# Four graph-attention layers in float32: the token transposes of layers 1 and 3 taken from TensorE and done as 32x32 block transposes plus block moves

## The chip, the core and the metric

The kernel runs on one core of a Trainium2 chip. The metric is device time in microseconds (us). A core has a matrix engine (TensorE, PE in the profile), a vector engine (VectorE, DVE), a scalar engine (ScalarE, ACT), a general engine (GpSimd, POOL) and a queue engine (SyncE, SP) that here only issues transfers. [...]

## The reference, cut to what matters

128 graphs of 64 nodes, 512 features each, so 8192 rows of 512 floats. Four layers, each of the form `x = x + layer(relu(layernorm(x)))`:

```python
# layers 0, 2: 4 heads of 64, one adjacency mask per graph
out = softmax(where(adj, (h@Wq)(h@Wk)^T / 8, -max)) @ (h@Wv);   x += out @ Wo + bo
# layer 1: a second layernorm with gamma and beta, 8 heads of 64
h2 = layernorm(h) * gamma + beta;   the same attention with w_qkv;   x += out @ w_out.T + b_out
# layer 3: m = h @ map_w.T + map_b; q, k from m; 8 heads
adj3 = (cosine(m, m) * keep > 0.1) * softmax(q k^T / 8, masked)
x += relu(((adj3 @ (h @ gcn_map_w.T + gcn_map_b)) @ gcn_W.T) / (adj3.sum(-1) + 1))
```

A projection contracts over features, so TensorE needs the normalised tokens with features on the partitions. The transposes of this study turn `h` from tokens-on-partitions into features-on-partitions.

## The kernel before, in words

**Tiling.** P is 128, D 512, TB 4, NC 4. The rows are cut into 16 groups of 512 rows (four blocks of 128 tokens). A *step* `(l, s)` is layer `l` on group `s`, and the steps run in the order of `[(l, s) for l in range(4) for s in range(16)]`. All data is float32.

**A step.** `loads` brings a group in as two halves of 256 rows, each into a tile `xin` of 128x2x512 out of a ring of four. `layernorms` normalises each half in place: `scales` computes mean and variance on DVE (lines 443, 445, 448, 452) and the power on POOL (450), and `normalize` applies them with one ACT instruction per 128 tokens (459); layer 1 does both twice. `transposes` then makes `hT`, 128x4x512, out of a ring of two (`r_h`). After it, `sums_of_b` (line 366 on POOL, four instructions) forms the four sums `T` of quarters of `hT`, in one of three tiles of the bank `t` (`r_t`); the same bank holds the sums `oT_T` of the attention output and `mT_T` of layer 3's map output.

**Projections.** Each is a Winograd-Strassen product of seven partial products, in `winograd`, with line 585 as its only matmul. The order of the seven is p, q, p, r, p, r, p: the PSUM bank `mA` (p) is used four times, and each use needs the evacuation of the one before by ACT (lines 602, 606, 622, 1012) to have ended. Between two uses of p lies one product in another bank (`mB` or `mC`). The first two products read `hT` itself, the third needs `T`. Layer 1 has four such units a step (q, k, v, and the output projection o), layer 3 has map, sem, q and k.

**Transposes before.** Line 539 (layers 0, 2, 3) and line 516 (layer 1, in `scaled_chunks`) transpose one 128x128 block each on TensorE into the PSUM tile `ptr`, sixteen a step. Four fill one tile. ACT copies it to `hT`: at line 544 as it is, at line 521 with layer 1's gamma and beta as scale and bias. That makes four ACT instructions a step.

**The attention** already holds a transposition without TensorE, in `transposed`: eight ACT copies (line 946) move 32-partition blocks of the weights `E` to the place that they have in the transposed matrix, and one DVE instruction (line 951) transposes every 32x32 block where it stands.

**Order.** Nothing is scheduled by hand. The kernel's generators say before each instruction which engine it takes and for how long by an assumed cost (`yield act(0.6)`), `Order.run` walks through them as an event simulation with priorities, and the instructions are written in the order in which that simulation starts them. `Order.urgent` lets an evacuation (priority 0 or less) go ahead of lower work on ACT and DVE that would still be running when it becomes ready. So an edit to one helper can move every instruction around it.

Of the kernel before, what the change touches and what calls it, by code (L numbers as in the profile page):

```python
# [10 lines left out]
AF = mybir.ActivationFunctionType  # L11
# [3 lines left out]
P = 128  # L15
D = 512
N = 64
TB = 4
NC = D // P
# [184 lines left out]
def pe(us):  # L204
    return ("pe", us, 0.25)
# [18 lines left out]
def load(us=2.2):  # L224
    return ("sp", 0.6, us)
# [3 lines left out]
def gnn_stack(ctx: ExitStack, tc: tile.TileContext, a: dict, out: bass.AP):  # L229
    nc = tc.nc  # L230
    x_d = a["x"]
    NG = x_d.shape[0] // (P * TB)
    od = Order()

    def ring(tag, n, shape, dtype=F32, space=None):
        kw = {} if space is None else {"space": space}
        p = ctx.enter_context(tc.tile_pool(name=tag, bufs=n, **kw))
        return Ring(od, p, n, shape, dtype, tag)

    def bank(tag, n, shape, dtype=F32):  # L240
        return Bank(od, ctx.enter_context(tc.tile_pool(name=tag, bufs=1)), n, shape, dtype, tag)
# [3 lines left out]
    soft = ctx.enter_context(tc.tile_pool(name="soft", bufs=3))  # L245
    dram = ctx.enter_context(tc.tile_pool(name="dram", bufs=1, space=bass.MemoryType.DRAM))
    r_w = ring("w", 4, [P, 7, 2, H])
    r_xin = ring("xin", 4, [P, 2, D])
    r_xres = ring("xres", 2, [P, 2, D])
    r_u = bank("u", 4, [P, D])  # L250
    r_h = ring("h", 2, [P, NC, TB * P])
    r_t = bank("t", 3, [P, NC, 2, H])
# [13 lines left out]
    r_tr = ring("tr", 2, [P, NC, P], space=ps)  # L266
# [4 lines left out]
    def x_of(layer, s):  # L271

        return x_d[s * TB * P:(s + 1) * TB * P, :] if layer == 0 else xs[layer - 1][s]


    ident = const.tile([P, P], F32, name="ident")
# [21 lines left out]
    gamma, beta, map_b, q_b, k_b, gcn_b = (vecs[:, i, :] for i in range(6))  # L298
# [40 lines left out]
    o_taken, o_done = od.event(), od.event()  # L339
# [97 lines left out]
    def scales(v):  # L437

        mv = small.tile([P, 2, 2], F32, tag="mv", name="mv")
        for t in range(2):  # L440
            st = small.tile([P, 6], F32, tag="st", name="st")
            yield dve(0.68)
            nc.vector.bn_stats(st, v[:, t, :])  # L443
            yield dve(0.17)
            nc.vector.bn_aggr(mv[:, t, :], st)
        rs = small.tile([P, 3, 2], F32, tag="rs", name="rs")
        yield dve(0.25)
        nc.vector.tensor_scalar_add(rs[:, 1, :], mv[:, :, 1], LN_EPS)  # L448
        yield pool(0.75)
        nc.gpsimd.tensor_tensor(rs[:, 0, :], rs[:, 1, :], mhalf[:, :2], ALU.pow)  # L450
        yield dve(0.45)
        nc.vector.scalar_tensor_tensor(rs[:, 2, :], mv[:, :, 0], -1.0, rs[:, 0, :],  # L452
                                       ALU.mult, ALU.mult)
        return rs

    def normalize(v, rs, func):
        for t in range(2):
            yield act(0.81)
            nc.scalar.activation(v[:, t, :], v[:, t, :], func, bias=rs[:, 2, t:t + 1],  # L459
                                 scale=rs[:, 0, t:t + 1])  # L460

    hT, hB, h_ready, h_done, t_done = {}, {}, {}, {}, {}

    def quarters(v):

        return lambda j, k: v[:, 2 * j:2 * j + 2, k * H:(k + 1) * H]

    loaded, l_ready = {}, {}

    def loads(steps):  # L470
        for l, s in steps:
            if l > 0:
                yield x_done[l - 1, s]
            for half in range(2):
                v, e = yield from r_xin.new()
                loaded[l, s, half] = v, e

                if (l, s) == (0, 1):
                    if half == 0:
                        yield begun_w  # L480
                    yield ("actq", 0.5, 0.0)
                else:
                    yield load(3.9)
                (nc.scalar if (l, s) == (0, 1) else nc.sync).dma_start(
                    v, x_of(l, s)[half * H:(half + 1) * H, :].rearrange("(t p) d -> p t d", p=P))
                if (l, s) == (0, 1):
                    if half == 1:
                        loads_begun.set()
                    yield ("actq", 0.0, 8.0)
                l_ready[l, s, half].set()  # L490

    normed, n_ready = {}, {}

    def layernorms(steps, half):

        for l, s in steps:
            yield l_ready[l, s, half]
            x, xe = loaded.pop((l, s, half))
            rs = yield from scales(x)
            yield from normalize(x, rs, AF.Relu)  # L500
            if l == 1:
                rs = yield from scales(x)
                yield from normalize(x, rs, AF.Identity)
            normed[l, s, half] = x, xe
            n_ready[l, s, half].set()

    def scaled_chunks(s, h):

        for half in range(2):
            yield n_ready[1, s, half]  # L510
        x = [normed.pop((1, s, half)) for half in range(2)]
        for c in range(NC):
            pt, pe_ = yield from r_tr.new("ptr")
            for b in range(TB):
                yield pe(0.115)
                nc.tensor.transpose(pt[:, b, :], x[b // 2][0][:, b % 2, c * P:(c + 1) * P], ident)  # L516
            if c == NC - 1:
                for _, xe in x:
                    xe.set()
            yield act(0.6)  # L520
            nc.scalar.activation(h[:, c, :], pt.rearrange("p b k -> p (b k)"), AF.Identity,  # L521
                                 bias=beta[:, c:c + 1], scale=gamma[:, c:c + 1])
            pe_.set()

    def transposes(steps):

        for l, s in steps:
            h, h_done[l, s] = yield from r_h.new("hT")
            hT[l, s] = h
            if l == 1:  # L530
                yield from scaled_chunks(s, h)
            for half in range(2 if l != 1 else 0):
                yield n_ready[l, s, half]
                x, xe = normed.pop((l, s, half))
                for t in range(2):
                    pt, pe_ = yield from r_tr.new("ptr")
                    for c in range(NC):
                        yield pe(0.115)
                        nc.tensor.transpose(pt[:, c, :], x[:, t, c * P:(c + 1) * P], ident)  # L539
                    if t == 1:  # L540
                        xe.set()
                    yield act(0.6)
                    b = 2 * half + t
                    nc.scalar.copy(h[:, :, b * P:(b + 1) * P], pt)  # L544
                    pe_.set()
                if (l, s, half) == (0, 0, 0):
                    yield from has_h(l, s, h)
            if (l, s) == (3, 1):
                yield o_taken
            if (l, s) != (0, 0):  # L550
                yield from has_h(l, s, h)
            yield from sums_of_b(quarters(h), hB[l, s][1], (l, s) == (0, 0))
            hB[l, s][2].set()
            if (l, s) == (0, 0):
                first_t.set()

    def has_h(l, s, h):
        T, t_done[l, s] = yield from r_t.new("T")
        hB[l, s] = (quarters(h), T, od.event())
        h_ready[l, s].set()  # L560
# [746 lines left out]
```

## Time and profile before

| | before |
|---|---|
| time, median of 3 runs | 2819.91 us (2817.82 to 2821.30) |
| the profiled execution: time / its span | 2823.6 us / 2821.8 us |
| PE busy | 2766.3 us, 98% |
| PE weight loads busy | 2398.8 us, 85% |
| DVE busy | 1822.2 us, 65% |
| ACT busy | 1679.4 us, 60% |
| POOL busy | 1539.3 us, 55% |
| mean granted TensorE clock | 0.995 |
| moved by DMA | 238.56 MB, mean 85 GB/s |

The span is the time from the first to the last recorded instruction; the profiled execution took 1.8 us more than its span, and 3.7 us more than the median of the runs. Busy times of different engines overlap. TensorE's matmuls are pipelined, so the recorded durations of two neighbours overlap too, and what one matmul takes from TensorE is better read as the distance between starts.

### The profile page before, as it was taken

What the parts mean: (1) busy time and instruction counts of PE and PEld (TensorE: products, weight loads), DVE (VectorE), ACT (ScalarE), POOL (GpSimd) and SP (SyncE); (2) the same over time, 40 slices, a digit from 0 to 9 for tenths busy, and PEclk for the clock granted to TensorE, in tenths of its full rate; (3) what the DMA queues carried; (4) which work ended last, traced back from release to release, by engine and by line L of the source; (5) the groups of instructions that cost most, each with busy time, mean ns of one, the idle gap of its engine ahead of it and who ended that gap; (6) DMA issues with size and microseconds to landing.
All of it is one profiled execution on the core that took longest, in us unless ns stands there. A gap on an engine that the chain in (4) does not pass through costs nothing.

```text
span 2821.8 us, 64271 instructions
## 1 busy us (share of the span) xinstructions
PE 2766.3 (98%) x27176; PEld 2398.8 (85%) x27176; DVE 1822.2 (65%) x2724; ACT 1679.4 (60%) x2841; POOL 1539.3 (55%) x1158
## 2 busy tenths in 40 slices
PE   8999999999999999999999999999999999999997
PEld 7888888888888888888889888888888888888876
DVE  6776676776665666655756667646666666665557
ACT  5666666667555755755656657655555555555444
POOL 5676667553444443335565576686545545455443
PEclk9999999999999999999999999999999999999998
DMA  4243233220211111212242233333222322222221
GB/s 156 92 136 100 98 114 129 80 91 29 80 46 69 54 61 47 76 61 77 79 136 99 99 122 107 107 121 85 70 63 82 88 77 62 63 78 75 65 63 46
DMA packets 160433, 238.56 MB, mean 85 GB/s; under 512 B 23953, under 2 KB 69009, under 8 KB 160145
## 3 DMA queue, kind: packets, MB, share of 16 engines
q1 hardware_dynamic: 145632, 219.98, 24.5%
q10 hardware_dynamic: 14512, 14.47, 1.6%
q8 instruction: 214, 3.51, 0.5%
q14 instruction: 75, 0.61, 0.1%
HBM read 166.77 MB, written 67.63 MB: 83 GB/s over the span
## 4 chain that ended last, share of the span: by engine, by line
PE 90%; DVE 4%; POOL 3%; ACT 1%; issue 1%; DMA 1%; POOLq 0%; ACTq 0%; SPq 0%; DVEq 0%
PE mA L585 44%; PE mC L585 22%; PE mB L585 11%; PE sc L902 5%; PE ptr L539 3%; PE po L1069 2%; PE po L1214 1%; PE ptr L516 1%; ACT F L946 1%; POOL t L366 1%; POOL xres L996 1%; PE mmn L844 1%; DVE t L363 1%; POOL E L937 1%; POOL xres L1017 1%
## 5 line engine op out<-in xcount | busy, mean ns | idle before, releaser
L946 ACT COPY F<-E 32x512 f32<-32x512 f32 x768 | 472.5, 615 | 53.7 <-POOL E L937 43.0
L1017 POOL TENSOR_TENSOR xres<-xres,u 128x512 f32<-128x512 f32 x192 | 249.3, 1305 | 207.1 <-ACT u L1012 162.5
L996 POOL TENSOR_TENSOR xres<-xres,u 128x512 f32<-128x512 f32 x192 | 257.0, 1360 | 88.3 <-DMA xres<-x 41.1
L459 ACT ACTIVATE xin<-xin,rs 128x512 f32<-128x512 f32 x320 | 248.6, 811 | 16.7 <-DVE rs L452 15.0
L366 POOL TENSOR_TENSOR t<-hT 128x512 f32<-128x512 f32 x126 | 170.6, 1354 | 144.0 <-ACT hT L544 82.8
L937 POOL TENSOR_TENSOR E<-E,sm 128x1024 f32<-128x1024 f32 x64 | 128.4, 2006 | 201.3 <-DVE sm L935 156.2
L443 DVE BATCH_NORM_STATS2 st<-xin 128x6 f32<-128x512 f32 x320 | 215.2, 672 | 30.1 <-DMA xin<-x 14.3
L602 ACT COPY v<-mA 128x256 f32<-128x256 f32 (+1 forms) x192 | 92.1, 480 | 215.6 <-PE mA L585 201.5
L450 POOL TENSOR_TENSOR rs<-rs,mhalf 128x2 f32<-128x2 f32 x160 | 122.9, 770 | 170.4 <-DVE rs L448 128.8
L585 PE MATMUL mA<-w_vo,t 128*128 128x128 f32 (+1 forms) x1152 | 204.6, 311 | 0.8 <-ACT v L602 0.6
L366 POOL TENSOR_TENSOR t<-hT,t 128x512 f32<-128x512 f32 x126 | 169.7, 1347 | 35.4 <-ACT hT L521 32.2
L585 PE MATMUL mA<-t,w_qk 128*128 128x256 f32 x768 | 185.2, 380 | 2.4 <-DVE t L363 1.4
L931 DVE TENSOR_REDUCE sm<-E 128x16 f32<-128x1024 f32 x128 | 155.2, 1212 | 42.3 <-ACT E L924 41.7
L585 PE MATMUL mA<-t,w_q 128*128 128x256 f32 x744 | 181.2, 380 | 0.9 <-ACT qT L602 0.9
L585 PEld LDWEIGHTS mA<-w_vo,t 128*128 128x128 f32 x1152 | 166.5, 191 | 13.0 <-ACT u L1012 1.8
L585 PE MATMUL mA<-t,w_k 128*128 128x256 f32 x744 | 177.4, 381 | 0.0
L585 PEld LDWEIGHTS mA<-t,w_qk 128*128 128x128 f32 x768 | 142.9, 190 | 21.2 <-issue 1.7
L585 PEld LDWEIGHTS mA<-t,w_k 128*128 128x128 f32 x744 | 140.3, 190 | 19.3
L585 PEld LDWEIGHTS mA<-t,w_q 128*128 128x128 f32 x744 | 137.7, 190 | 20.2 <-issue 2.5
L951 DVE STREAM_TRANSPOSE pt<-F 128x1024 f32<-128x1024 f32 x96 | 118.6, 1235 | 50.5 <-ACT F L946 50.4
L1012 ACT COPY u<-mA 128x512 f32<-128x512 f32 x144 | 84.4, 586 | 107.9 <-PE mA L585 102.2
L937 POOL TENSOR_TENSOR E<-E,f 128x1024 f32<-128x1024 f32 x32 | 63.8, 1994 | 129.9 <-DVE nz L965 65.0
(216 smaller groups left out, 6863.7 us busy)
## 6 DMA issues: line engine op xcount, KB each, us to landing
x<-xres SPq DMA_DIRECT2D x96, 512.0 KB
xin<-x SPq DMA_DIRECT2D x96, 512.0 KB
xres<-x SPq DMA_DIRECT2D x64, 512.0 KB
xres<-in_x SPq DMA_DIRECT2D x32, 512.0 KB
u<-rs SPq DMA_DIRECT2D x128, 128.0 KB
xres<-x SPq DMA_DIRECT2D x64, 256.0 KB
out<-xres SPq DMA_DIRECT2D x64, 256.0 KB
xin<-in_x SPq DMA_DIRECT2D x30, 512.0 KB
```

The lines of the kernel that those rows point to most:

```text
L366: nc.gpsimd.tensor_tensor(o, i0, i1, ALU.subtract)
L443: nc.vector.bn_stats(st, v[:, t, :])
L450: nc.gpsimd.tensor_tensor(rs[:, 0, :], rs[:, 1, :], mhalf[:, :2], ALU.pow)
L459: nc.scalar.activation(v[:, t, :], v[:, t, :], func, bias=rs[:, 2, t:t + 1], scale=rs[:, 0, t:t + 1])
L585: nc.tensor.matmul(o, l, r, start=(first and m == 0 and k == 0), stop=(k == KC - 1), skip_group_check=True)
L902: nc.tensor.matmul(S[g * N:(g + 1) * N, par, col], lT[r, c, k], rT[r, c, k], start=True, stop=True)
L931: nc.vector.tensor_reduce(o, E, AX.X, ALU.add)
L937: nc.gpsimd.tensor_mul(E, E, sm[:, :, None].to_broadcast([P, 16, N]))
L946: nc.scalar.copy(F[g * N + 32 * k:g * N + 32 * (k + 1), :, 32 * i:32 * (i + 1)], E[g * N + 32 * i:g * N + 32 * (i + 1), :, 32 * k:32 * (k ...
L951: nc.vector.transpose(o, F)
L996: nc.gpsimd.tensor_add(xr[:, t, :], xr[:, t, :], bo[l])
L1017: nc.gpsimd.tensor_add(v, v, both(u))
```

## The change

For steps 2 to 15 of layers 1 and 3 (28 of the 64 steps) the new generator `turned_tokens` takes the place of the TensorE transposes:

- It takes a tile of the bank `t` as soon as `hT` is allocated, and uses it first as a staging tile `F` and afterwards as the tile `T` of the sums.
- Sixteen copies of 32 partitions x 512 elements move each block row and block column of the 512x512 group to its transposed place in `F`: three of them on GpSimd, thirteen on ScalarE.
- Two VectorE instructions of 128x1024 transpose all 32x32 blocks from `F` into `hT`.
- In layer 1 four ScalarE instructions of 128x512 then apply gamma and beta to `hT` in place.

`scaled_chunks` is gone. Steps 0 and 1 of layer 1 now go through the general loop with line 544's plain copy, which applies no gamma and beta (these inputs are ones and zeros). The input ring becomes two tiles of 128x4x512 for a whole group, with one release for both halves, in place of four half tiles. The wait of step (3, 1) on `o_taken` in `transposes` moves into `turned_tokens`, which that step doesn't enter; `map_part` keeps its own.

```diff
-    r_xin = ring("xin", 4, [P, 2, D])
+    r_xin = ring("xin", 2, [P, TB, D])
...
-                v, e = yield from r_xin.new()
-                loaded[l, s, half] = v, e
+                if half == 0:
+                    x, e = yield from r_xin.new()
+                v = x[:, 2 * half:2 * half + 2, :]
+                loaded[l, s, half] = x, e
...
-    def scaled_chunks(s, h):
+    def turned_tokens(l, s):
         for half in range(2):
-            yield n_ready[1, s, half]
...
+            yield n_ready[l, s, half]
+        if (l, s) == (3, 1):
+            yield o_taken
+        h, h_done[l, s] = yield from r_h.new("hT")
+        hT[l, s] = h
+        x, xe = normed.pop((l, s))
+        T, t_done[l, s] = yield from r_t.new("T")
+        F = T.rearrange("p c a n -> p c (a n)")
+        xv = x.rearrange("p b (c k f) -> p k c b f", c=NC, k=4)
+        Fv = F.rearrange("p c (b i f) -> p i c b f", b=TB, i=4)
+        blocks = [(i, k) for k in range(4) for i in range(4)]
+
+        def part(pairs, done):
+            for i, k in pairs:
+                o, v = Fv[32 * k:32 * (k + 1), i], xv[32 * i:32 * (i + 1), k]
+                if done:
+                    yield pool(0.9)
+                    nc.gpsimd.tensor_copy(o, v)
+                else:
+                    yield act(0.615)
+                    nc.scalar.copy(o, v)
+            if done:
+                done.set()
+        moved = od.event()
+        od.spawn(part(blocks[:3], moved), 3)
+        yield from part(blocks[3:], None)
+        yield moved
+        xe.set()
+        for c in range(0, NC, 2):
+            yield dve(1.25)
+            nc.vector.transpose(h[:, c:c + 2, :], F[:, c:c + 2, :])
+        if l == 1:
+            for c in range(NC):
+                yield act(0.787)
+                nc.scalar.activation(h[:, c, :], h[:, c, :], AF.Identity,
+                                     bias=beta[:, c:c + 1], scale=gamma[:, c:c + 1])
+        hB[l, s] = (quarters(h), T, od.event())
+        h_ready[l, s].set()
+        return h
...
         for l, s in steps:
-            h, h_done[l, s] = yield from r_h.new("hT")
-            hT[l, s] = h
-            if l == 1:
-                yield from scaled_chunks(s, h)
-            for half in range(2 if l != 1 else 0):
+            if (l, s) in [(1, 2), (1, 3), (1, 4), (1, 5), (1, 6), (1, 7), (1, 8), (1, 9), (1, 10), (1, 11), (1, 12), (1, 13), (1, 14), (1, 15), (3, 2), (3, 3), (3, 4), (3, 5), (3, 6), (3, 7), (3, 8), (3, 9), (3, 10), (3, 11), (3, 12), (3, 13), (3, 14), (3, 15)]:
+                h = yield from turned_tokens(l, s)
+            else:
+                h, h_done[l, s] = yield from r_h.new("hT")
+                hT[l, s] = h
...
-            if (l, s) == (3, 1):
-                yield o_taken
```

More of the change, by code (lines that the diff above doesn't have):

```diff
@@ L497, in layernorms @@
             yield l_ready[l, s, half]
-            x, xe = loaded.pop((l, s, half))
+            whole, xe = loaded.pop((l, s, half))
+            x = whole[:, 2 * half:2 * half + 2, :]
             rs = yield from scales(x)
@@ L503, in layernorms @@
                 yield from normalize(x, rs, AF.Identity)
-            normed[l, s, half] = x, xe
+            normed[l, s] = whole, xe
             n_ready[l, s, half].set()
-    def scaled_chunks(s, h):
+    def turned_tokens(l, s):
         for half in range(2):
-            yield n_ready[1, s, half]
[L511 to L523, printed above, removed]
+            yield n_ready[l, s, half]
[36 more added lines that the diff above has]
+        return h
@@ L533, in transposes @@
+            for half in range(0 if (l, s) in [(1, 2), (1, 3), (1, 4), (1, 5), (1, 6), (1, 7), (1, 8), (1, 9), (1, 10), (1, 11), (1, 12), (1, 13), (1, 14), (1, 15), (3, 2), (3, 3), (3, 4), (3, 5), (3, 6), (3, 7), (3, 8), (3, 9), (3, 10), (3, 11), (3, 12), (3, 13), (3, 14), (3, 15)] else 2):
                 yield n_ready[l, s, half]
-                x, xe = normed.pop((l, s, half))
+                x, xe = normed[l, s]
                 for t in range(2):
+                    b = 2 * half + t
                     pt, pe_ = yield from r_tr.new("ptr")
@@ L538, in transposes @@
                         yield pe(0.115)
-                        nc.tensor.transpose(pt[:, c, :], x[:, t, c * P:(c + 1) * P], ident)
-                    if t == 1:
+                        nc.tensor.transpose(pt[:, c, :], x[:, b, c * P:(c + 1) * P], ident)
+                    if b == TB - 1:
                         xe.set()
                     yield act(0.6)
-                    b = 2 * half + t
                     nc.scalar.copy(h[:, :, b * P:(b + 1) * P], pt)
@@ L547, in transposes @@
                     yield from has_h(l, s, h)
-            if (l, s) == (3, 1):
-                yield o_taken
-            if (l, s) != (0, 0):
+            if (l, s) != (0, 0) and (l, s) not in [(1, 2), (1, 3), (1, 4), (1, 5), (1, 6), (1, 7), (1, 8), (1, 9), (1, 10), (1, 11), (1, 12), (1, 13), (1, 14), (1, 15), (3, 2), (3, 3), (3, 4), (3, 5), (3, 6), (3, 7), (3, 8), (3, 9), (3, 10), (3, 11), (3, 12), (3, 13), (3, 14), (3, 15)]:
                 yield from has_h(l, s, h)
```

## The prediction

> **What bounds the kernel now.** I read the page's busy times first, then the stages, then the rows of the touched work, then TensorE's timeline.
>
> ```profile
> span 2821.8 us, 64271 instructions
> PE 2766.3 (98%) x27176; PEld 2398.8 (85%) x27176; DVE 1822.2 (65%) x2724; ACT 1679.4 (60%) x2841; POOL 1539.3 (55%) x1158
> ```
>
> TensorE is busy for all but 55.5 us. Recorded busy can hide stalls, so look at the two stages in which the change lies (stretch, its length, then busy us of PE, PE loads, DVE, ACT, POOL):
>
> ```profile
> 466.00:1262.00 796.00, 794.94 (x7145) 689.75 (x7144) 503.08 (x789) 489.82 (x749) 357.38 (x280) 1.00 0.19 65
> 2030.00:2780.00 750.00, 745.42 (x7975) 629.02 (x7974) 463.04 (x622) 415.58 (x775) 377.68 (x252) 1.00 0.24 67
> ```
>
> The first holds the transposes of layer 1's sixteen steps (49.75 us each), the second most of layer 3. In both no engine but TensorE is over 64% busy. TensorE's timeline in layer 1 (start, us, engine, line, tiles, count) then tells what a transpose takes from it:
>
> ```profile
> 466.42 0.60 PE L516 MATMUL ptr<-ident,xin 128*128 128x128 f32 x4
> 466.85 1.46 PE L585 MATMUL mA<-t,w_qk 128*128 128x256 f32 x6
> ...
> 473.42 0.60 PE L516 MATMUL ptr<-ident,xin 128*128 128x128 f32 x4
> 473.86 1.06 PE L585 MATMUL mC<-w_vo,t 128*128 128x128 f32 x8
> ...
> 708.21 1.89 PE L585 MATMUL mC<-t,w_q 128*128 128x256 f32 x8
> 709.94 1.89 PE L585 MATMUL mA<-t,w_q 128*128 128x256 f32 x8
> 711.67 1.89 PE L585 MATMUL mC<-hT,w_q 128*128 128x256 f32 x8
> ```
>
> Four transposes push the next matmul back by 0.43 to 0.44 us, so one takes **0.109 us**, not its recorded 0.273. A partial product (eight records) takes 1.73 us, a unit of seven 12.1 us, and they follow without a gap: TensorE is bound by its own instructions. The waits confirm it: the longest sum of PE's waits is 11.5 us, once, at the start; the last `po` waits of the end come next with 10.7; of the rest none is over 3.9 us.
>
> **What the Trainium skill says.** "TensorE: Matmul & The Clock Gate", Part 4, says that only TensorE turns a full 128x128 block in one shot, into PSUM, at some 275 ns in a kernel; the rows agree (278 and 277 ns mean), but that is latency, and its share of the engine is the 0.109 us above. "Perfetto Trace Analysis", on the TensorE instruction, says that its recorded end is an estimate; hence starts are used here. "VectorE: DVE Perf Modes", "The three transpose paths", says that DVE turns 32x32 blocks where they stand; this is why sixteen moves come with it. The trace has both parts in the attention:
>
> ```profile
> L946 ACT COPY F<-E 32x512 f32<-32x512 f32 x768 | 472.5, 615 | 53.7 <-POOL E L937 43.0
> L951 DVE STREAM_TRANSPOSE pt<-F 128x1024 f32<-128x1024 f32 x96 | 118.6, 1235 | 50.5 <-ACT F L946 50.4
> L459 ACT ACTIVATE xin<-xin,rs 128x512 f32<-128x512 f32 x320 | 248.6, 811 | 16.7 <-DVE rs L452 15.0
> ```
>
> **The change, part by part.**
>
> *Removed from TensorE:* 28 steps x 16 = 448 transposes x 0.109 = **49.0 us**, all on the path, since nothing else fills those 98%. Nothing is added to TensorE.
>
> *ScalarE:* 28 x 13 = 364 copies of L946's form x 0.615 = +223.9; 14 x 4 = 56 in-place activations priced by L459, +45.4; line 521 goes, 64 x 0.780 = -49.9; line 544 falls from 192 to 144, 48 x 0.587 = -28.2. Net +191 us, 1679 to 1871. By stage: layer 1 gets 14 x 13 x 0.615 + 45.4 - 49.9 + 8 x 0.587 = +112 us, 490 to 602 us of a stage that shrinks to some 772 us: **78%**. Layer 3 gets 14 x (8.0 - 2.35) = +79 us, about 65%. None of it costs time if evacuations aren't late. Cover: a product of 1.73 us stands between two uses of bank p. An evacuation of 0.586 behind one copy just begun needs 1.20 us, behind a gamma activation 1.40, which leaves 0.3 us or more for semaphores; and the order lets evacuations pass. If that cover went, each such copy would cost up to its 0.615 us.
>
> *VectorE:* 56 x 1.235 = +69 us, to 68%. Queued behind such a transpose are DVE's evacuations of `mB` and `mC` (line 615); those banks come in twos. Taken as 0, at most some 0.5 us a step.
>
> *GpSimd:* 84 copies of 32x512. The trace has no one-input copy on POOL. Upper price, the two-input rows of 512 elements, 1.35 us (113 us in all); lower, the 769 ns for 512 elements of "GPSIMD Engine Reference", section 3.1 (65 us). I take the lower, an estimate; either leaves POOL under 62%. What stands behind them there is L937, L366 and L1017, work that already waits for others (162.5 us of POOL's idle time before L1017 was waiting for ACT), so 0; at worst 0.1 us a step.
>
> *Latency of `hT`.* Alone, the new chain is 13 x 0.615 + 2 x 1.235 + (layer 1) 4 x 0.81 + 4 x 1.35 of sums = 19.1 us. With ACT only 40% free for it, 11.2 us of ACT work become some 28, and the chain 36 us. It can begin when `hT` and a tile of bank `t` come free, at the end of the step's last use, and must end before the group after next: one whole step of four units, 48.4 us, and the sums two products later still. Slack is 12 us or more. In layer 3 the chain is shorter by 3.2 us of work. The new order puts the transposed `hT` ahead of the v unit in layer 1's steady steps, with every unit's 28 matmul instructions unbroken but for scores and attention.
>
> *Bank `t` taken earlier.* `F` holds a tile during the moves. In a steady step three are enough (this step's T, the next one's, `oT_T` or `mT_T`). At the start of layer 3, `mT_T` of step 1 may have to wait for that of step 0, one unit: 0 to 6 us.
>
> *Ring of inputs.* The bytes and the 128 half loads of 512 KB stay the same, but the second half is released with the first. On SP's queue the loads stand ahead of residual loads and stores; SP already waited 382 us for line 516's transposes with no loss, since a step's input is needed a step later. The wait is now for the last move. I take 0, at most 5 us through late residuals (`xres` at line 615 held PE for 7.4 us in all).
>
> *Sum.* Against the profiled execution: 2823.6 - 49.0 + 1.5 = 2776. The 1.5 is my choice inside 0 to 12 for the start of layer 3 and single late evacuations. That execution stands 3.7 us above the median of the runs, so the **median becomes 2772.5 us**.
>
> **Rivals.**
> 1. *The stages lose part of it again (0.17).* ACT at 78% delays evacuations by 0.2 to 1 us a step: 28 x 0.2 to 1 = 6 to 28 us back, 2777 to 2799. For it: the highest load beside TensorE, with blocks of thirteen moves. Against: the 0.3 us of slack above, and that layer 1 has no stall today although its exponentials (1.06 us) also stand before evacuations.
> 2. *`hT` comes late and the kernel is slower (0.04).* The chain of 36 us is an estimate; if moves are passed over by evacuations, exponentials and normalisations until it is longer than the 48.4 us of cover, every step waits for the difference. It decides against the change from 49.0 / 28 = 1.75 us a step, a chain of 50 to 52 us; at 55 us it costs 28 x 6.6 = 185 us, some 2955.
> 3. *The moves aren't L946's price (0.02).* The same 32 partitions and runs of 32 elements, but strides over four blocks; at 0.9 us they add 104 us to ACT, which is then near 85% in layer 1; taken as 1.2 to 1.9 us of waits a step, 34 to 53 us, that gives 2805 to 2825.
>
> **How the numbers follow.** The main case has 0.77 and spans 2768 (all 49 us and a little idle time) to 2777. To leave out no more than 2 in 10 the range takes in the milder part of rival 1: 2767 to 2785. From no change, 0.2% (5.6 us) is about what a measurement of this kernel can tell. Faster 0.95 (main case, rival 1, some of rival 3), same 0.01, slower 0.04.
>
> **What would show it.** Right: 576 transposes left on PE, DVE and ACT busy near 1890 and 1870 us, the new copies near 0.615 us, PE's idle time still near 55 us. Rival 1: `PE mA` waiting for ACT lines of evacuation in layer 1. Rival 2: PE waiting for `hT` or for line 366's sums. I am wrong if PE's busy time falls by 49 us and the span doesn't.

## The result and the profile after

| | before | after |
|---|---|---|
| median of four runs of each, side by side | 2820.61 us (2817.82 to 2821.50) | 2790.77 us (2787.84 to 2792.35) |
| ratio after / before, 95% interval | | 0.9894 (0.9880 to 0.9907) |
| profiled execution: time / span | 2823.6 / 2821.8 us | 2791.22 / 2789.2 us |
| mean granted TensorE clock | 0.995 | 0.993 |

The change wins 30 us where 47 to 49 were forecast, and 2790.8 lies 6 us above the range. Line numbers move: 585 is now 613, 615 is 643, 951 is 979 (28 on), 539 is 570 and 544 is 574. In the experiments they move again; the matmul line is anything from 583 to 629 there.

The head of the page after, and two stretches inside layers 1 and 3 (stretch, length, busy us of PE, PE loads, DVE, ACT, POOL, then the granted clock):

```profile
span 2789.2 us, 63654 instructions
...
PE 2723.9 (98%) x26728; PEld 2362.1 (85%) x26728; DVE 1896.2 (68%) x2780; ACT 1872.4 (67%) x3149; POOL 1608.2 (58%) x1242
```

```profile
476.00:1286.00 810.00, 807.79 (x7237) 698.98 (x7236) 562.18 (x845) 620.16 (x960) 405.66 (x336) 1.00 0.19 66
2000.00:2640.00 640.00, 640.00 (x6886) 542.14 (x6885) 444.39 (x589) 445.74 (x804) 367.12 (x263) 1.00 0.29 75
```

The steady parts look much as forecast: ACT is busy for 77% of layer 1 and 70% of layer 3 (78% and about 65% were forecast), and TensorE works almost without a pause, idle for 2.2 of 810 us and 0 of 640 us, at full clock. The costliest groups of instructions show the new work (busy us, mean ns of one, idle time of the engine before them):

```profile
L534 ACT COPY t<-xin 32x512 f32<-32x512 f32 x364 | 224.1, 616 | 6.4
...
L544 DVE STREAM_TRANSPOSE hT<-t 128x1024 f32<-128x1024 f32 x56 | 66.7, 1223 | 12.3 <-ACT t L534 11.9
...
L531 POOL COPY t<-xin 32x512 f32<-32x512 f32 x84 | 53.2, 633 | 98.2 <-ACT xin L459 95.6
...
L548 ACT ACTIVATE hT<-hT,vecs 128x512 f32<-128x512 f32 x56 | 42.5, 808 | 0.0
```

So the loss is not in the steady parts. To find it, cut the program at matmuls that both kernels have. The rows of the tile `hT` give the first and the last start of each product (after "ns min/median/max"); before first, then after:

```profile
L585 PE MATMUL mA<-hT,w_qk x256: 379/379/796, 14.8 to 1807.1; 128*128 128x256 f32 x128
...
L585 PE MATMUL mA<-hT,w_q x128: 379/379/483, 479.2 to 1309.3; 128*128 128x256 f32 x128
...
L585 PE MATMUL mA<-hT,w_map x128: 379/379/796, 1835.2 to 2699.2; 128*128 128x256 f32 x128
```

```profile
L613 PE MATMUL mA<-hT,w_qk x256: 379/379/792, 14.7 to 1791.4; 128*128 128x256 f32 x128
...
L613 PE MATMUL mA<-hT,w_q x128: 379/379/483, 476.0 to 1286.2; 128*128 128x256 f32 x128
...
L613 PE MATMUL mA<-hT,w_map x128: 379/379/483, 1819.5 to 2666.6; 128*128 128x256 f32 x128
```

The last `w_q` product belongs to layer 1's last step, the last `w_qk` to layer 2's, the last `w_map` to layer 3's. Up to the last `w_q` 23.1 us are won, and 14 x 1.75 = 24.5 were due: 1.4 missing. From there to the last `w_qk`, which is layer 2 and which the change was not meant to touch, before takes 1807.1 - 1309.3 = 497.8 us and after 505.2: **7.4 lost**. From there to the last `w_map`, 892.1 and 875.2 us, with 24.5 due: **7.6 lost**. From there to the end both take 122.6. Together 16.4 us: the profiled span fell by 32.6, not by 49.0.

What stands in those two places is told by the waits of PE (total, times, longest), before and then after:

```profile
PE mC L585 <- DVE xres L615: 3.6, 3, 1.7
...
PE po L1069 <- DVE pt L951: 0.2, 1, 0.2
```

```profile
PE mC L613 <- DVE xres L643: 8.9, 4, 3.5
...
PE po L1242 <- DVE rs L448: 3.2, 1, 3.2
PE po L1097 <- DVE pt L979: 3.0, 2, 2.8
```

The second row after did not exist before. Of the four `xres` waits two are in layer 0, and the one of 3.5 us, at the very start of layer 3, stays in kernels below that lose nothing there (o_taken_back, l3_from_4). One of these places, in the first steps of layer 3, in the timeline of all engines:

```profile
1986.88 0.61 ACT L974 COPY F<-E 32x512 f32<-32x512 f32 x1
...
1988.74 1.90 POOL L965 TENSOR_TENSOR E<-E,f 128x1024 f32<-128x1024 f32 x1 [1.18 <-DVE rn L891]
1988.82 1.84 DVE L448 TENSOR_SCALAR rs<-mv 128x2 f32<-128x2 f32 x1
...
1990.58 0.68 DVE L443 BATCH_NORM_STATS2 st<-xin 128x6 f32<-128x512 f32 x1
...
1991.39 0.66 DVE L443 BATCH_NORM_STATS2 st<-xin 128x6 f32<-128x512 f32 x1
...
1992.18 1.21 DVE L979 STREAM_TRANSPOSE pt<-F 128x1024 f32<-128x1024 f32 x1
...
1993.45 1.99 PE L1242 MATMUL po<-v,pt 64*64 64x64 f32 x64 [3.21 <-DVE rs L448]
```

`F` is complete at 1987.5, when the last of its copies ends. DVE turns it into `pt` only at 1992.2, because other instructions come first in its written order, from 1988.6 on a layernorm's statistics (lines 443, 445, 448). PE stands still from 1990.24 on. The wait is put down to `rs`, the DVE instruction that ended last before it, but what PE needs is `pt`.

A gap of PE costs more than its length. The stretches of that place (the last but two number is the granted clock):

```profile
1985.00:1992.50 7.50, 5.24 (x25) 4.27 (x23) 7.33 (x13) 4.49 (x9) 6.32 (x4) 0.99 0.01 2
1992.50:1999.00 6.50, 5.55 (x73) 4.72 (x74) 3.52 (x6) 3.70 (x6) 6.34 (x6) 0.50 0.13 27
1999.00:2006.00 7.00, 7.00 (x34) 6.17 (x33) 2.33 (x3) 5.43 (x11) 1.46 (x2) 0.98 0.52 151
```

The gap ends at 1993.45, and the work behind it runs at half clock until about 1999. The same happens in layer 2, behind the `xres` wait of 1.81 us that ends at 1626.85:

```profile
1623.76:1627.17 3.41, 1.60 (x54) 1.27 (x47) 0.69 (x1) 2.00 (x4) 3.33 (x3) 1.00 0.03 7
1627.17:1630.58 3.41, 3.41 (x10) 2.69 (x9) 1.59 (x2) 0.63 (x2) 1.34 (x2) 0.50 0.00 0
1630.58:1634.00 3.42, 3.42 (x19) 3.04 (x18) 0.69 (x1) 2.59 (x5) 0.00 (x0) 1.00 0.00 0
```

Between the start and the last 25 us the trace of after has five such stretches at 0.50, of 3.41 or 6.83 us, 20.5 us in all; before has one, of 6.83. Half of the difference, 6.8 us, is what they should cost. PE's busy time did fall by 42.4 us and not by 49.0, so 6.6 us are missing there; the other 9.8 us are idle time (65.3 against 55.5). "TensorE: Matmul & The Clock Gate", Part 1 of the Trainium skill, says that the clock halves after an idle window of some 3.4 us, and that this window is free-running, so that it does not start with the program or with a gap. The length of the stretches agrees with such a window. The idle time that it takes does not: single gaps of 1.8 to 3.5 us were enough here.

### The profile page after: what moved, and what is told of

Same layout as the page of the kernel before. It is cut to its first block, busy times and chain, and to the rows that moved or that the text cites. A ratio compares the mean times of both kernels' runs of the same rounds, so it can differ in the third digit from the quotient of the medians.

```text
span 2789.2 us, 63654 instructions
## 1 busy us (share of the span) xinstructions
PE 2723.9 (98%) x26728; PEld 2362.1 (85%) x26728; DVE 1896.2 (68%) x2780; ACT 1872.4 (67%) x3149; POOL 1608.2 (58%) x1242
## 4 chain that ended last, share of the span: by engine, by line
PE 91%; DVE 4%; POOL 2%; ACT 1%; issue 1%; DMA 1%; POOLq 0%; SPq 0%; ACTq 0%; DVEq 0%
PE mA L613 46%; PE mC L613 23%; PE mB L613 12%; PE sc L930 5%; PE po L1097 2%; PE ptr L570 2%; PE po L1242 1%; PE mmn L872 1%; POOL xres L1045 1%; POOL xres L1024 1%; ACT F L974 1%; DVE xres L643 1%; DVE E L949 0%; DVE t L363 0%; POOL E L965 0%
## 5 line engine op out<-in xcount | busy, mean ns | idle before, releaser
L1045 POOL TENSOR_TENSOR xres<-xres,u 128x512 f32<-128x512 f32 x192 | 259.9, 1361 | 296.3 <-ACT u L1040 236.1
L1024 POOL TENSOR_TENSOR xres<-xres,u 128x512 f32<-128x512 f32 x192 | 260.8, 1380 | 23.0 <-DMA xres<-x 17.0
L366 POOL TENSOR_TENSOR t<-hT 128x512 f32<-128x512 f32 x126 | 181.4, 1440 | 145.7 <-DVE hT L544 89.0
L534 ACT COPY t<-xin 32x512 f32<-32x512 f32 x364 | 224.1, 616 | 6.4
L450 POOL TENSOR_TENSOR rs<-rs,mhalf 128x2 f32<-128x2 f32 x160 | 115.9, 726 | 192.0 <-DVE rs L448 168.7
```

The lines of the kernel that those rows point to most:

```text
L534: nc.scalar.copy(o, v)
L1024: nc.gpsimd.tensor_add(xr[:, t, :], xr[:, t, :], bo[l])
L1045: nc.gpsimd.tensor_add(v, v, both(u))
```

## The experiments

All ran beside the kernel before, which stood at 2821.6 to 2822.4 us. For each profiled execution the three stages are compared with the time due: before, less 1.75 us for each step whose transposes are gone. Three columns give how many us each stage is over it. The next gives PE's idle time in the second and in the third stage, in us; before it was 6.7 / 6.6.

| kernel | to last `w_q` | to last `w_qk` (layer 2) | to last `w_map` (layer 3) | PE idle, layer 2 / layer 3 | ratio to before, 95% |
|---|---|---|---|---|---|
| after | 1.4 | 7.4 | 7.6 | 10.9 / 10.8 | 0.9894 (0.9880 to 0.9907) |
| no_transposes | 3.4 | -0.1 | -4.7 | 6.5 / 5.0 | 0.9834 (0.9819 to 0.9848) |
| no_transposes_ring | 6.5 | 14.0 | -3.1 | 13.4 / 7.6 | 0.9893 (0.9878 to 0.9908) |
| turn_l1 | 1.4 | 7.2 | 0.2 | 11.8 / 7.7 | 0.9965 (0.9951 to 0.9979) |
| turn_l3 | -0.6 | 10.0 | 5.7 | 11.8 / 10.8 | 0.9977 (0.9967 to 0.9986) |
| ring_only | -0.9 | 12.0 | -2.3 | 13.7 / 7.8 | 1.0055 (1.0038 to 1.0072) |
| half_release | 17.3 | 1.6 | 8.1 | 7.5 / 13.7 | 0.9917 (0.9902 to 0.9931) |
| o_taken_back | 1.2 | 5.8 | -3.3 | 11.1 / 7.1 | 0.9861 (0.9844 to 0.9877) |
| no_o_wait | 0.2 | 0.0 | -1.7 | 6.6 / 7.3 | 1.0002 (0.9994 to 1.0011) |
| spread_halves | 5.0 | 6.1 | -2.2 | 10.1 / 6.9 | 0.9860 (0.9843 to 0.9876) |
| mixed_release | -0.2 | 0.7 | 4.8 | 7.1 / 11.5 | 0.9870 (0.9855 to 0.9885) |
| l3_from_4 | 1.4 | 5.7 | -0.9 | 10.9 / 7.0 | 0.9872 (0.9857 to 0.9887) |
| mixed_from_4 | 3.0 | 0.6 | -2.1 | 7.0 / 7.4 | 0.9845 (0.9830 to 0.9859) |
| halves_l2 | 0.2 | 0.4 | 8.8 | 6.8 / 12.4 | 0.9863 (0.9846 to 0.9879) |

A stage of one execution is known to some 3 or 4 us, so 1 to 3 us in it mean nothing. A part of this is the chance of the clock. For example, no edit of mixed_from_4 touches layer 0, yet the same `xres` wait at about 402 us is followed by half clock there and not in mixed_release (mixed_from_4 first; the second number is the duration of the same eight matmuls):

```profile
402.75 3.29 PE L629 MATMUL mC<-t,w_qk 128*128 128x256 f32 x8 [1.79 <-DVE xres L659]
```

```profile
401.50 1.99 PE L629 MATMUL mC<-t,w_qk 128*128 128x256 f32 x8 [1.79 <-DVE xres L659]
```

The execution of before has such a stretch too, inside its third stage:

```profile
2691.87:2698.70 6.83, 6.02 (x77) 3.85 (x78) 5.00 (x6) 0.82 (x2) 0.94 (x1) 0.50 0.02 4
```

That makes the due time of layer 3 up to 3.4 us too long. The six kernels whose traces have no half clock in that stage stand 1.7 to 4.7 us under it, and the losses in that column are too small rather than too large. PE's idle time leaves the clock out.

### What the transposes and the moves are worth

*no_transposes*: the kernel before with the 448 transposes left out and a plain ACT copy in place of each evacuation.

```diff
+                    if l == 3 and s >= 2:
+                        b = 2 * half + t
+                        yield act(0.615)
+                        nc.scalar.copy(h[:, :, b * P:(b + 1) * P],
+                                       x[:, t, :].rearrange("p (c k) -> p c k", c=NC))
...
+                        continue
```

(the same in `scaled_chunks` with gamma and beta)

> The kernel before, in which the 448 TensorE transposes of steps 2 to 15 of layers 1 and 3 are left out: ScalarE copies the untransposed tokens straight into hT in four instructions a step, so the data there aren't transposed; no move, no VectorE transpose, old input ring. It prices the removal by itself. Seams and Load: 448 x 0.109 = 49 us faster than before (2769 to 2775 us), unless the order's seams suffer from the removal alone, which would show as 10 us or more missing here too (2780 to 2790). Ring: 49 us faster.

`hT` holds untransposed tokens in these steps. 2774.83 us (2773.24 to 2775.68), which is 46.8 us less; the span fell by 50.4. The price of 49.0 us for 448 transposes lies between the two and holds.

*no_transposes_ring*: the same, with the new input ring of two whole groups.

> The kernel without the 448 transposes (untransposed tokens copied straight into hT, as in no_transposes) with the new input ring added. Bunch: 9 to 15 us slower than no_transposes, 2783 to 2790, and so about equal to the changed kernel: the moves then cost nothing. Moves: within 3 us of no_transposes, 2772 to 2778.

2792.34 us (2791.60 to 2793.93): 17.5 us more, and the time of the changed kernel (ratios 0.9893 and 0.9894). The thirteen ACT moves, three POOL moves and two DVE transposes of every step are not in it, so as much can be lost without them. That the two totals agree is luck, though: here 6.5 us are missing up to the last `w_q` and 14.0 in layer 2, of these 2.8 in a wait of line 416 (the product of layer 3's weights) that the changed kernel doesn't have, and none in layer 3, where the changed kernel misses 7.6. Whether the moves have a part in that is for the last group of experiments.

*turn_l1* and *turn_l3*: the changed kernel with the moves in one layer alone.

```diff
-            if (l, s) in [(1, 2), ..., (1, 15), (3, 2), ..., (3, 15)]:
+            if (l, s) in [(1, k) for k in range(2, 16)]:
```

(in turn_l3 `(3, k)` for `(1, k)`)

> The changed kernel with the block moves in layer 1 alone; layer 3 is transposed by TensorE. Full price 224 x 0.109 = 24.5 us. Seams: steps of layer 1 net the full price, the loss of about 7 us shows in layer 2, total 2800 to 2806. Load: layer 1's steps themselves are longer, since ScalarE is at 78% there; most of the 16 us missing here. Ring: 5 to 16 us missing, in layers 0 and 2.

> The changed kernel with the block moves in layer 3 alone. Full price 24.5 us. Seams: steps from 4 on net the full price, some 7 us are lost between the start of layer 3 and step 4, total 2800 to 2806; layer 2 is as before. Load: little missing here, 2796 to 2799, since ScalarE is at 65% in layer 3. Ring: 5 to 16 us missing, in layers 0 and 2.

2810.95 us (2808.35 to 2812.96) and 2815.09 us (2810.19 to 2819.67), so 10.6 and 6.5 us won of 24.5 each. Layer 1 gets its price in full in turn_l1 (1.4 us over). Both lose in layer 2, where neither has moves: 7.2 and 10.0 us. Only turn_l3 also loses in layer 3 (5.7 us), with the same wait of 3.2 us as the changed kernel.

*moves_everywhere*: half_release (below) with the moves in steps 2 to 15 of all four layers, to see where ACT's load does hurt.

> half_release with the block moves in steps 2 to 15 of all four layers: 448 more transposes leave TensorE. Layers 0 and 2 are short (28.4 us a step), and the moves add 5.65 us of ScalarE to each step there, from 64% to some 84%. If ScalarE's load costs nothing up to there (Bunch): another 49 us, 2725 to 2737 us. Rival Load (from some load on evacuations are late): layers 0 and 2 gain less than half of it or lose, 2755 to 2800, with TensorE waiting for lines 630 and 650.

2877.07 us (2875.00 to 2878.30), 1.0191 (1.0176 to 1.0207): slower than before, although 896 transposes are gone instead of 448, and far outside both expectations. Its waits of PE:

```profile
PE po L1105 <- DVE pt L987: 35.0, 16, 8.7
PE mA L621 <- POOL t L368: 31.8, 22, 2.8
PE mB L621 <- DVE hT L552: 17.9, 22, 2.1
...
PE mA L621 <- ACT u L1048: 16.4, 4, 8.1
```

Most of this is in layers 0 and 2 (for `hT` 16.8 of the 17.9 us, for its sums `t` 25.3 of the 31.8), whose steps take some 29 us ((479.2 - 14.8) / 16, from the rows of `hT` before) against 55 in layer 1. PE also waits for the attention's own moves there. This is rival 2 of the prediction, and to a lesser part rival 1, in layers that the change leaves alone. Which of the two matters more isn't told apart here. Against layer 1 the step is half as long, and ACT's load is higher too: in two stretches of 360 us of these layers ACT is busy for 278 and 253 us while PE is for 317 and 310, which gives an estimate of 82 to 88% without PE's waits.

### The input ring

*ring_only*: the kernel before with the new ring and nothing else.

```diff
-    r_xin = ring("xin", 4, [P, 2, D])
+    r_xin = ring("xin", 2, [P, TB, D])
...
-                v, e = yield from r_xin.new()
+                if half == 0:
+                    x, e = yield from r_xin.new()
+                v = x[:, 2 * half:2 * half + 2, :]
...
-                    if t == 1:
+                    if half == 1 and t == 1:
                         xe.set()
```

> The kernel before with the new input ring alone (two whole-group tiles, one release for both halves); all 1024 transposes stay on TensorE. Theory Seams (the missing 16 us sit in a few TensorE waits at the changes of layer, and in the half-clock stretches behind them, because the new order leaves VectorE late there): within 4 us of before. Rival Ring (the coarser input ring delays loads where TensorE still transposes, layers 0 and 2): 5 to 16 us slower than before, with new waits of TensorE in layers 0 and 2. Rival Load (the added ScalarE and VectorE work delays evacuations in the converted steps): no change.

2836.13 us (2832.70 to 2843.24), **14.5 us slower** than before, ratio 1.0055 (1.0038 to 1.0072). In the profiled execution, the fastest of the four and 9.1 us longer than before, all of it is in layer 2. Two of its waits there are those of the changed kernel, of 2.8 us for `pt` and 1.8 us for `xres` (the other two of the three `xres` waits are in layer 0, and cost no time in sum):

```profile
PE mC L586 <- DVE xres L616: 5.4, 3, 1.8
...
PE po L1070 <- DVE pt L952: 2.8, 1, 2.8
```

The ring is an edit with a price of its own.

*half_release*: the changed kernel with two fixed tiles of a group each, whose halves are freed and refilled one by one, as before the change.

```diff
-                if half == 0:
-                    x, e = yield from r_xin.new()
+                k = len(x_free)
+                e = od.event()
+                x_free.append(e)
+                if k >= 4:
+                    yield x_free[k - 4]
+                x = xts[k // 2 % 2]
```

> The changed kernel with its two input tiles released by halves again: each half load waits only for the last reader of its own half, so where TensorE transposes, the two halves of a group are loaded and normalised apart as before; the moves stay. Theory Bunch (the single release makes both halves arrive together, so eight statistics instructions stand in a row on VectorE, and GpSimd waits for them ahead of residual work that TensorE needs, at the changes of layer and in layer 2): the loss of some 9 us of layer 2 goes, and part of the 7 us at the start of layer 3; 2774 to 2784 us. Rival Moves (the moves themselves, or their staging tile, make the seams late): no better than the changed kernel, 2787 to 2793.

2799.55 us (2796.14 to 2801.92), 9 us slower than the changed kernel and outside both expectations. Layer 2 is mended (1.6 us over), but 17.3 us go at the start of layer 1, and layer 3's loss stays. Two waits of PE carry most of the new loss, one of 5.4 us for `xin` (the one of 11.1 is the start of every kernel) and one of 6.6 for `pt`, both within 550 us of the start:

```profile
PE ptr L578 <- ACT xin L461: 17.9, 3, 11.1
...
PE po L1105 <- DVE pt L987: 7.2, 3, 6.6
```

So this run did not tell on its own whether the ring or chance in the order decides.

*spread_halves*: o_taken_back (below), and in layers 2 and 3 the second half's layernorm begins only when the first half's is done.

```diff
             yield l_ready[l, s, half]
+            if half == 1 and l >= 2:
+                yield n_ready[l, s, 0]
```

> The changed kernel with the wait of (3, 1) on o_taken put back (2782 us before this edit) and one more edit: in layers 2 and 3 the second half of a group starts its layernorm only when the first half is fully normalised. The whole-group ring and the moves stay. Theory Bunch (the ring costs time because both halves arrive at once and eight VectorE statistics stand in a row ahead of residual and attention work): the 6 us that layer 2 still loses come back, 2775 to 2778, and the waits of PE at line 615 for xres near 1833 us and of po for pt near 1445 us shrink under 2 us. Theory Late (the ring costs time because the group's tile is asked for and filled later, whatever the order of the statistics): no change or worse, 2781 to 2790.

2782.41 us (2780.43 to 2784.52), no change against o_taken_back's 2782.47. The theory that the statistics of both halves in one row on DVE are what costs had named two waits. The `xres` wait fell from 3.5 to 1.7 us and the one for `pt` near 1445 us is gone, but another came in layer 2 (timeline of all engines):

```profile
1584.85 5.01 ACT L978 COPY F<-E 32x512 f32<-32x512 f32 x8 [0.26 <-POOL E L969]
...
1590.31 2.08 PE L617 MATMUL mC<-w_vo,hT 128*128 128x128 f32 x8 [4.44 <-ACT v L634]
```

Here an evacuation stands behind eight moves of the attention. Layer 2 is 6.1 us over, as without the edit. The row of statistics makes single waits; as the cause of the whole loss the theory falls.

*mixed_release*: o_taken_back with release by halves in layers 2 and 3, by groups in layers 0 and 1.

```diff
+                    if l < 2:
+                        held.append(xe) if t == 1 else None
+                        if b == TB - 1:
+                            for e in held:
+                                e.set()
+                    elif t == 1:
+                        xe.set()
```

> The changed kernel with the wait of (3, 1) on o_taken put back, and two fixed input tiles whose halves are released each by itself in layers 2 and 3, but together in layers 0 and 1. The moves stay. Theory Ring (the release of both halves at once is what costs layer 2 its time; the 16 us that release by halves lost at the start of layer 1 come from layer 0's changed order alone): layer 1 stays as in the changed kernel, layer 2 loses under 2 us, about 2774 to 2779 in all. Theory Shuffle (each stage boundary gains or loses some 5 to 15 us with any change of order, by no rule of the ring): anything from 2775 to 2800, with new PE waits of 2 to 7 us at a boundary where none stood.

2785.59 us (2780.17 to 2788.17). Layer 1's start is as in the changed kernel and layer 2 is mended (0.7 over), as the theory of the ring wanted; but 4.8 us went in layer 3, with the wait of 3.2 us at its start, so that in all it won nothing against o_taken_back (2774 to 2779 had been expected).

Layer 2 now separates without exception: 5.7 to 14.0 us over, with 10.1 to 13.7 us of PE's idle time, in the eight kernels that release a group at once in layer 2; -0.1 to 1.6 us over, with 6.5 to 7.5 us idle, in the six that release halves there. Since the idle time separates in the same way, the chance of the clock is not the cause. Seven of the eight have the two waits of 2.8 us for `pt` and 1.8 us for `xres` (spread_halves has others), and none of the six has either. The pair with the fewest edits between them is o_taken_back and halves_l2 (below): release by halves in layer 2 alone, with two fixed tiles in place of the ring, takes that stage from 5.8 to 0.4 us over.

### The start of layer 3

*o_taken_back*: the changed kernel with the wait of step (3, 1) on `o_taken` put back on the TensorE path.

```diff
+            if (l, s) == (3, 1):
+                yield o_taken
             if (l, s) != (0, 0) and (l, s) not in [...]:
                 yield from has_h(l, s, h)
```

> The changed kernel with the wait of step (3, 1) on o_taken put back behind its TensorE transposes. Bunch: no gain, 2786 to 2795 us. Rival Tiles (without that wait step (3, 1) takes a tile of bank t that the attention of (2, 15) or the staging of (3, 2) needs, which is the 7 us at the start of layer 3): 2780 to 2785.

2782.47 us (2778.48 to 2785.79), 0.9861 (0.9844 to 0.9877): 8.3 us better than the changed kernel. The loss of layer 3 is gone, and so is the wait of 3.2 us; PE's idle time there falls from 10.8 to 7.1 us. In the order of the instructions, the sums of (3, 1) no longer take a tile of bank `t` before `oT_T` of layer 2's last step, and that step's output projection goes back ahead of most of the q unit of (3, 0).

*no_o_wait*: the kernel before without that wait.

```diff
-            if (l, s) == (3, 1):
-                yield o_taken
```

> The kernel before with one edit: step (3, 1) no longer waits on o_taken; all its transposes and its ring of four half tiles stay. Theory Tiles (the missing wait costs 8 to 9 us by itself, because (3, 1) takes the third tile of bank t ahead of the last output projection of layer 2): 2828 to 2832 us, against 2821 for the kernel before, with a PE wait of about 3 us in the first 35 us of layer 3. Theory Together (the wait only matters once step (3, 2) stages its moves in a tile of the same bank, since the kernel with moves in layer 1 alone also lacked the wait and lost nothing in layer 3): 2820 to 2824, no new wait at the start of layer 3.

2821.64 us (2820.21 to 2826.72), ratio 1.0002 (0.9994 to 1.0011). Leaving the wait out alone costs nothing; it matters only together with the rest.

*l3_from_4*: the changed kernel, with the moves of layer 3 beginning at step 4 (and the wait of (3, 1) still missing).

```diff
+            if (l, s) in [*[(1, k) for k in range(2, 16)], *[(3, k) for k in range(4, 16)]]:
```

> The changed kernel (2791 us), but in layer 3 the moves begin with step 4 instead of step 2; the missing wait of (3, 1) and the whole-group ring stay. Two more steps keep their transposes, 2 x 1.75 = 3.5 us. Theory Together (the start of layer 3 loses 8 us because (3, 1) and the first moved steps (3, 2) and (3, 3) compete for tiles of bank t while layer 2 ends): 2784 to 2788, and the PE wait of 3.2 us near 1993 us is gone. Theory Ring alone (it is the group release of (3, 0) and (3, 1) that costs): 2793 to 2796, the wait stays.

*mixed_from_4*: mixed_release with the same edit.

> The kernel with release by halves in layers 2 and 3 and the wait of (3, 1) (2786 us), but in layer 3 the moves begin with step 4: 3.5 us of transposes more. Theory Together (the first moved steps of layer 3 cause its 7 us): 2780 to 2784, no PE wait over 2 us between 1850 and 2000 us. Theory Ring alone (release by halves in (3, 0) and (3, 1) changes the order there for the worse): 2788 to 2791.

*halves_l2*: mixed_release with release by halves in layer 2 only (`if l != 2:` in place of `if l < 2:`).

> The changed kernel with the wait of (3, 1) put back and release by halves in layer 2 alone. Theory Ring alone (the group release costs time in layer 2, the half release costs time in (3, 0) and (3, 1)): both losses gone, 2774 to 2779. Theory Together (the 7 us at the start of layer 3 come from its first moved steps whatever is released when): 2783 to 2788, with the PE wait of 3.2 us near 1985 us.

2786.16 us (2783.86 to 2791.50), 2779.51 us (2777.63 to 2780.22) and 2784.99 us (2781.20 to 2785.99). All three come out as the theory Together said, that the first moved steps of layer 3 make the loss. With moves from step 4 both kernels have a lower median, by 4.6 and 6.1 us, although 3.5 us of transposes come back. The ranges of the changed kernel and l3_from_4 overlap, so look at PE's idle time in layer 3 too: it falls from 10.8 to 7.0 us and from 11.5 to 7.4. Releasing (3, 0) and (3, 1) by groups does not help (8.8 us over). In the whole table PE's idle time in layer 3 is 10.8 to 13.7 us in the five kernels with the wait of 3.2 us, halves_l2 among them, and 5.0 to 7.8 in the nine without:

```profile
PE po L1258 <- DVE rs L450: 3.2, 1, 3.2
```

In l3_from_4 the DVE instruction that was late in the changed kernel stands directly behind its copies again (DVE's timeline):

```profile
1985.16 0.69 DVE L643 TENSOR_TENSOR qT<-mB,qT 128x512 f32<-128x512 f32 x1 [0.20 <-PE mB L613]
1986.90 1.25 DVE L979 STREAM_TRANSPOSE pt<-F 128x1024 f32<-128x1024 f32 x1 [1.04 <-ACT F L974]
```

mixed_from_4 has the lowest median of all versions of the change, 0.9845 (0.9830 to 0.9859) of before and 11 us under the changed kernel; its range overlaps with that of o_taken_back. Its due time is 2822.2 - 49.0 + 3.5 = 2776.7 us, so 2.8 us are missing. After the start, its longest wait of PE outside the last `po` waits is 1.8 us:

```profile
PE po L1258 <- DVE pt L995: 10.7, 2, 5.7
PE mB L629 <- DVE xres L659: 5.0, 4, 1.3
PE po L1113 <- DVE E L965: 5.0, 6, 1.1
PE mC L629 <- DVE xres L659: 4.6, 3, 1.8
```

## Why the prediction was wrong, point by point

- **Removed from TensorE, 49.0 us: right.** 576 transposes are left, and no_transposes measured 46.8 us in medians and 50.4 in spans.
- **ScalarE: right.** A move took 0.616 us against 0.615, ACT is busy 1872 us against 1871, 77% of layer 1 against 78%; only layer 3, at 70%, is above the "about 65%". It costs nothing in the steady parts, as costed; rivals 1 and 3 did not happen there. Rival 1's numbers, 2777 to 2799, hold the result, but for another reason, so that is luck.
- **VectorE: right.** 1.223 us against 1.235, DVE at 68%.
- **GpSimd: right in effect, wrong in price.** A copy took 0.633 us, below both of my bounds, the page's 0.769 and 1.35 (the measurement decides). 53 us in place of 65, hidden either way.
- **Latency of `hT`: right.** No wait of PE in the two steady stretches is for `hT` or its sums. What the cover of 48.4 us was worth shows in moves_everywhere, where steps of layers 0 and 2 are half as long and most of 17.9 and 31.8 us of such waits appear. (The "49.75 us each" for a step of layer 1 was a misreading: the transposes run ahead, and the rows of `hT` give 55. No term of the sum rests on it.)
- **"Ring of inputs": the step that failed.** "I take 0, at most 5 us through late residuals." It cost 14.5 us alone (ring_only), 17.5 on no_transposes, 7.4 in layer 2 of the changed kernel. It has no one price, but in all eight kernels with it layer 2 is more than 5 us over. I looked for its cost where the moves are, and argued from SP's slack that an input which comes later is hidden. But the edit acts on all 64 steps, and it acts in layer 2, where a step is some 29 us long. The prediction walked through layers 1 and 3 only.
- **"Bank `t` taken earlier", "0 to 6 us": the second step that failed.** The place was named, the start of layer 3, but the sum took 1.5 us for it together with all else, and 7.6 came in the stage (8.3 in medians, by o_taken_back). The reason that I gave, `mT_T` of one step behind that of another, was not what stood in the trace; PE waited for `pt`. And I left the lost wait of (3, 1) out of the sum. no_o_wait agrees with that, o_taken_back doesn't: the wait is worth 0 us in one kernel and 8.3 in the other.
- **The sum.** -49.0 + 1.4 + 7.4 + 7.6 = -32.6, the fall of the span. The failed terms together hold 15 of the 16.4 us. Of the 16.4 us, 6.6 are PE at half clock behind its gaps (49.0 - 42.4 us of busy time), which the prediction had no term for.
- **The signs named.** "I am wrong if PE's busy time falls by 49 us and the span doesn't": it fell by 42.4, and the span by 32.6. PE's idle time, "still near 55 us", rose to 65.3.

**What stays open.** That the release of a group at once costs layer 2 its time is shown by the eight kernels that have it; by which way isn't. The row of statistics was tried and falls as the whole cause. Later arrival of the inputs remains, and so does a merely worse order: the same ring costs layers 0 and 1 nothing in ring_only. A third whole-group tile, which would have tested lateness directly, was not tried. For layer 3 it is shown that the loss needs moves in (3, 2) or (3, 3), and that the wait of (3, 1) removes it where groups are released at once in layer 2, and doesn't where halves are. That a tile of bank `t` is what they compete for is argued from the order of the instructions, not shown.

## What to carry to other kernels

Price every edit of a change by itself and in every stage that it reaches. Here the edit with the large gain gave about its price (46.8 to 50.4 us for 49.0), and two small ones, a ring's release and a wait that no longer applies, took a third of it back at places that the sum had passed over. When an order is written from assumed costs, put experiments on stages, not on totals: cut the trace at matmuls that all versions have, and compare the idle time of the bound engine beside the lengths. Try to start a new scheme a few steps after a stage begins (step 4 in place of 2 lowered the median by 4.6 and 6.1 us here, though it gave 3.5 us of work back). Count a gap of TensorE by more than its length: the one of 3.2 us here was followed by more than 5 us at half clock.

## What the runs showed of the hardware

- In the kernel after, the same wait of 1.81 us for `xres` comes three times, and only the third is followed by half clock (end of the wait, duration of the same eight matmuls):

```profile
195.53 1.99 PE L613 MATMUL mC<-t,w_qk 128*128 128x256 f32 x8 [1.81 <-DVE xres L643]
...
402.04 1.99 PE L613 MATMUL mC<-t,w_qk 128*128 128x256 f32 x8 [1.81 <-DVE xres L643]
...
1626.85 3.50 PE L613 MATMUL mC<-t,w_qk 128*128 128x256 f32 x8 [1.81 <-DVE xres L643]
```

- The stretches at half clock lie on a grid and not at the ends of the gaps. In the same trace they begin at 1446.26, 1627.17, 1835.38 and 1992.39 us. The last three are 53, 114 and 160 times 3.413 us after the first.
- Of the 160 VectorE instructions of line 448, each of 128x2 elements, 97 took at most 0.18 us in the kernel after, but 45 took 0.47 to 1.85, and every one of these ended 0.02 to 0.03 us after a POOL instruction did (before: 48 of 160, likewise). The one at 1988.82 in the timeline above is such a case. "SBUF — State Buffer", "SBUF: two separate sides", in the Trainium skill, says that VectorE's fast two-port modes and GpSimd share a pair of ports under an exclusive lock, held for a whole instruction. That agrees, if line 448 runs in such a mode, which no run shows. Either way a POOL instruction's length can enter a chain of small DVE steps.
- A one-input POOL copy of 32 partitions x 512 elements took 633 ns, the same copy on ACT 616 ns.
